# A four-layer graph kernel whose instruction order is planned: weight preparation put into the plan, and planned times as occupancies

## The chip, the cores and the metric

The kernel runs on one core of a Trainium2 chip. The metric is the device time of one execution in microseconds (us). All times below come from the profile of the kernel before, or from its timed runs.

## The reference

32 graphs of 512 nodes with 256 features pass through four layers, each followed by a residual and a layer norm over the features. Everything is float32. `A` is the weighted adjacency matrix (512 x 512) of a graph.

```python
# layer 0: a graph isomorphism layer
h = (1.0 + eps) * x + einsum('bnm,bmd->bnd', adj, x)
x = layernorm(x + relu(h @ W1 + b1) @ W2 + b2)
# layer 1: graph attention, 4 heads of 64
h = einsum('bnd,dhf->bnhf', x, W)
e = leaky_relu(e_dst[:, :, :, None] + e_src[:, :, None, :], 0.2)   # e_src, e_dst: h times a_src, a_dst
attn = softmax(where(adj > 0.5, e, -1e9))
x = layernorm(x + einsum('bhij,bjhf->bihf', attn, h) + bias)
# layer 2: attention, 8 heads of 32
scores = q k^T / sqrt(32) + log(adj + 1e-6)                          # q, k, v: x times Wq^T, Wk^T, Wv^T
x = layernorm(x + (softmax(scores) v) @ Wo^T + bo)
# layer 3: attention of x on itself, one head
s = (x @ W) x^T * adj, masked by the node mask
x = layernorm(x + softmax(s) x)
```

## The kernel before

**A plan.** Each graph is a list of some 330 steps. A step (class `Step`) has a name, an engine, a planned time in us, the steps that it comes after, the buffers that it takes, and a tiling mode of TensorE (`row`, `c32`, `c64`, or none). `Plan.order` plays a list schedule in advance, while the program is built: of the steps that can start first (within `ahead` us), it takes the one with the earliest due time. The due time of a step of graph g is `g * period` less the planned length of the longest chain behind it (`Plan.link`), plus `stay` times the planned cost of a change of tiling (table `CHANGE`). A planned time carries a hop after it: 0.2 us on TensorE, 0.05 on others (`HOP`). `Plan.run` tries 30 settings of `(period, ahead, window, stay)`, keeps the one whose plan ends first, and emits the steps in that order. Each engine then runs its own instructions in that order, and waits only where its operands demand it. The setting kept before is period 30, ahead 0.15, window 5, stay 100.

**Buffers.** 14 large ones (`B`, 8 KB per partition), 13 medium ones (`C`, 4 KB), and 8 PSUM banks (`p`). Counters in the same dictionary limit the number of graphs in a phase: `live` 5 graphs in all, `L0` to `L3` in the layers.

**The prologue** stands outside of the plan, and ahead of it (lines 244 to 365). ACT issues 24 DMAs for the weights; the four square weights are transposed on TensorE (L299) and evacuated by ACT (L304); DVE makes `selfw` (the identity times 1 + eps, L277) and the two extra columns of `wg_sb` (L284, L285); then two bounds are computed, one for the offsets of layer 1 (L311 to L327) and one from the Gram matrices of the q and k weights (L341 to L365). They decide at the end whether the result may be off limits, in which case a general path runs; with these inputs it doesn't. The temporaries of the prologue use the buffers C0 to C9.

**Steps of a graph**, by name, with the lines of the profile:

- layer 0: `at` transposes of A (L503), evacuated by ACT (`ate`, L511) and DVE (`atd`, L507); `h` (L535, `he` L542), `f` (L558, `fe` L564), `y` (L577), residual and norm `x1`, `st1` (L465, L423), `ve`, `dev`, `sh`, `r` (L436, L441, L446, L454).
- layer 1: `xt1` (L603), `v1` (L624, `ve1` L630), the bound offsets enter in `ab` (L638); the rows `R` go to DRAM and come back on all partitions as `R_bc` (`Rd`, L675); `z` (ACT, L714), `zm` (DVE, L725), `o1` (L748, mode c64); the sums of the weights through accumulating DMAs (L776) into `d1` (L794, c32); `yt` (L813 to L815), `yn`, `st2`.
- layer 2: `xt2` (L854), `q` and `k` (L873), `v2` (L891); for each of eight pairs of head group and column block, `s` (L910, mode row: 4 heads at once), `e` (ACT, L923), `m` (DVE, L932), `n` (L968, c32); the E tiles are added up by accumulating DMAs (`cd`, L943) into `d2` (L992, c32), whose reciprocal (`rc`, L1007) scales the output before `p` (L1040).
- layer 3: A is loaded again; `xt3`, `i` (L1079), `t` (L1093), `ta`, `tb` (DVE, L1107, L1113), `te` (ACT, L1121), `u` (L1138, `ue` L1147), `w` (L1165), `wx` (L1179), and the store.

Five graphs are under way at a time, so that TensorE's matmuls of one graph fill the waits of another.

Of the kernel before, what the change touches and what calls it, by code (L numbers as in the profile page):

```python
# [16 lines left out]
P = 128  # L17
# [28 lines left out]
class Plan:  # L46
# [6 lines left out]
    HOP = {"pe": 0.2}  # L53
# [19 lines left out]
    def step(self, name, eng, us, after=(), take=(), free=(), mode=""):  # L73


        def add(emit):
            steps = self.steps[-1]
            assert name not in steps and all(a in steps for a in after), (name, after)
# [17 lines left out]
    def link(self):  # L96

        self.left = []
        for steps, frees in zip(self.steps, self.frees):
            for name, s in steps.items():  # L100
                for a in s.after:
                    steps[a].then.append(name)
            for k, (_, after) in enumerate(frees):
                for a in after:
                    steps[a].frees.append(k)
            left = {}
            for name in reversed(steps):
                s = steps[name]
                left[name] = s.us + max(
                    (left[n] + self.HOP.get(s.eng, 0.05) for n in s.then), default=0.0  # L110
                )
            self.left.append(left)

    def order(self, period, ahead, window, stay):
# [9 lines left out]
        todo = [len(steps) for steps in self.steps]  # L124

        def open_to(n):
            nonlocal opened
            while opened < min(n, len(self.steps)):
                for name, s in self.steps[opened].items():
                    if not s.after:  # L130
                        ready[opened, name] = 0.0
                opened += 1

        open_to(window)
        while low < len(self.steps):
            found = []
            for (g, name), t in ready.items():
# [8 lines left out]
                else:  # L146
                    due = g * period - self.left[g][name] + stay * change
# [15 lines left out]
            end = ends[g][name] = t + s.us + (self.HOP.get(s.eng, 0.05) if s.eng else 0.0)  # L163
            last = max(last, end)
            out.append((g, name, t, got))
            for n in s.then:
                waits[g][n] -= 1
                if not waits[g][n]:
                    after = self.steps[g][n]
                    ready[g, n] = max(  # L170
                        ends[g][a] - (self.HOP.get(after.eng, 0.05) if after.eng == self.steps[g][a].eng and after.eng else 0.0)
                        for a in after.after
                    )
            for k in s.frees:
                fwaits[g][k] -= 1
                if not fwaits[g][k]:
                    key, after = self.frees[g][k]
                    kind, i = held[g].pop(key)
                    room[kind].append((max(ends[g][a] for a in after), i))
# [18 lines left out]
def fast_path(  # L198
# [39 lines left out]
    turn = [0]  # L238

    def bank_of(shape, name):  # L240
        turn[0] += 1
        return ps.tile(shape, F32, tag=f"p{turn[0] % 8}", name=name)

# [4 lines left out]
    nc.gpsimd.memset(nhalf, -0.5)  # L248
    ones = const.tile([P, P], F32, name="ones")
# [3 lines left out]

    w1_sb = const.tile([P, DC, DH], F32, name="w1_sb")
    nc.scalar.dma_start(w1_sb, w1.rearrange("(c p) f -> p c f", p=P))
    w2_sb = const.tile([P, HC, D], F32, name="w2_sb")
    nc.scalar.dma_start(w2_sb, w2.rearrange("(c p) f -> p c f", p=P))
    b1_sb = const.tile([P, HC], F32, name="b1_sb")
    nc.scalar.dma_start(b1_sb, b1.rearrange("(c p) -> p c", p=P))

    wg_sb = const.tile([P, DC, VW], F32, name="wg_sb")
    nc.scalar.dma_start(wg_sb[:, :, :D], wg.rearrange("(c p) h f -> p c (h f)", p=P))
    w3_sb = const.tile([P, DC, D], F32, name="w3_sb")
    nc.scalar.dma_start(w3_sb, w3.rearrange("(c p) f -> p c f", p=P))

    biases = dram.tile([3, NC, D], F32, tag="biases", name="biases", bufs=1)
    for k, b in enumerate((b2, gbias, bo)):
        for c in range(NC):
            nc.scalar.dma_start(biases[k, c : c + 1], bass.AP(b.tensor, b.offset, [[0, 1], [1, D]]))
    eps_bc = const.tile([P, 1], F32, name="eps_bc")  # L270
    nc.scalar.dma_start(eps_bc, row_bcast(eps0, 1))


    eps1 = const.tile([P, 1], F32, name="eps1")
    nc.vector.tensor_scalar_add(eps1, eps_bc, 1.0)
    selfw = const.tile([P, P], F32, name="selfw")
    nc.vector.tensor_scalar_mul(selfw, ident, eps1)  # L277

    for k, (name, a) in enumerate((("src", a_src), ("dst", a_dst))):
        a_bc = sb.tile([P, D], F32, tag=f"C{k}", name=f"a_{name}")  # L280
        nc.scalar.dma_start(a_bc, row_bcast(a, D))
        prod = sb.tile([P, DC, D], F32, tag=f"C{k+2}", name=f"wa_{name}_prod")
        for c in range(DC):
            nc.vector.tensor_mul(prod[:, c, :], wg_sb[:, c, :D], a_bc)  # L284
        nc.vector.tensor_reduce(  # L285
            wg_sb[:, :, D + k * H1 : D + (k + 1) * H1],
            prod.rearrange("p c (h f) -> p c h f", h=H1), AX.X, ALU.add,
        )


    wT = {}
    for i, (name, w) in enumerate((("q", wq), ("k", wk), ("v", wv), ("o", wo))):
        raw = sb.tile([P, DC, D], F32, tag=f"C{i+4}", name=f"w{name}_raw")
        nc.scalar.dma_start(raw, w.rearrange("(c p) f -> p c f", p=P))
        wT[name] = const.tile([P, DC, D], F32, name=f"w{name}T")
        pt = bank_of([P, N], f"w{name}_t")
        for ci in range(DC):
            for co in range(DC):
                nc.tensor.transpose(  # L299
                    pt[:, ci * D + co * P : ci * D + (co + 1) * P],  # L300
                    raw[:, co, ci * P : (ci + 1) * P],
                    ident,
                )
# [896 lines left out]
    for g in range(B):  # L1200
        graph(g)
# [475 lines left out]
```

## Time and profile before

| | |
|---|---|
| time, median of 3 runs | 3109.85 us (3102.59 to 3111.73) |
| span of the profiled run | 3097.9 us |
| TensorE matmuls (PE) | 2988.1 us busy, 15053 records |
| VectorE (DVE), ScalarE (ACT), GpSimd (POOL) | 2035.1, 1920.6, 617.1 us busy |
| DMA | 500.83 MB, mean 162 GB/s |
| mean granted clock of TensorE | 0.984 |
| first matmul of a graph starts at | 32.77 us |
| last matmul starts, its row's end | 3079.09, 3086.2 us |

A record of TensorE is one pass of a float32 matmul; a matmul of 512 columns is two. Busy times are unions: records that overlap count once. The time behind "idle before" is that in which the engine had nothing running, put down to what ended it. A release named "DMA" is a transfer's landing. Matmuls are pipelined, so a busy TensorE can still be losing time between two starts.

### The profile page before, as it was taken

To read this page: it belongs to the slowest core of one execution; us is meant where nothing else is said; L and a number is where in the kernel's file an instruction comes from. 1 tells how busy PE (TensorE), PEld (TensorE's weight loads), DVE (VectorE), ACT (ScalarE), POOL (GpSimd) and SP (SyncE) were. 2 spreads that over 40 slices of the span, in tenths; PEclk is the share of its full clock that TensorE was granted. 3 is DMA by queue.
4 is the path that set the end of the run, shared out by engine and by line. 5 is a ranking of instruction groups with operands and counts; after the bars stand their busy time and mean duration, and the time that the engine had idled before them with its cause. 6 is when DMAs were issued, how large, how long until landed. Compare 5 with 4: busy or idle time off the path is not lost.

```text
span 3097.9 us, 41135 instructions
## 1 busy us (share of the span) xinstructions
PE 2988.1 (96%) x15053; PEld 1698.5 (55%) x15053; DVE 2035.1 (66%) x3935; ACT 1920.6 (62%) x3849; POOL 617.1 (20%) x686
## 2 busy tenths in 40 slices
PE   6989999999999999999999999999999999999886
PEld 5545565555555555555555565555555555555443
DVE  1566666776576677666676666676576676666664
ACT  2656756666666566666666756666666567656552
POOL 1221221221122221122221121221221221122210
PEclk9999999999999999999999999999999999999898
DMA  4686877786877777777877877786877777776753
GB/s 133 146 182 143 169 171 155 174 174 159 182 157 162 172 162 180 167 148 169 179 162 171 170 170 155 177 171 154 179 164 162 167 167 177 175 149 147 175 124 69
DMA packets 160143, 500.83 MB, mean 162 GB/s; under 512 B 13504, under 2 KB 49088, under 8 KB 131264
## 3 DMA queue, kind: packets, MB, share of 16 engines
q0 software_dynamic: 78336, 352.36, 59.3%
q1 hardware_dynamic: 77824, 142.88, 13.6%
q10 hardware_dynamic: 3776, 2.90, 0.3%
q8 instruction: 121, 1.98, 0.2%
q14 instruction: 86, 0.70, 0.1%
HBM read 179.06 MB, written 17.05 MB: 63 GB/s over the span
## 4 chain that ended last, share of the span: by engine, by line
PE 75%; DMA 10%; ACT 9%; DVE 4%; issue 2%; ACTq 0%; POOL 0%; SPq 0%; POOLq 0%
PE s L910 8%; PE o_ps L1165 7%; PE o_ps L748 6%; PE hT_ps L535 6%; PE o_ps L968 6%; ACT z L714 6%; DMA R_bc<-R_dram 5%; PE y_ps L577 5%; PE v_ps L624 4%; PE kT_ps L873 4%; PE o2p_ps L1040 4%; PE iT_ps L1079 4%; PE v_ps L891 4%; PE qT_ps L873 4%; PE h1T_ps L558 3%; PE s L1093 3%
## 5 line engine op out<-in xcount | busy, mean ns | idle before, releaser
L932 DVE SCALAR_TENSOR_TENSOR z<-AT,z 128x1024 f32<-128x1024 f32 x512 | 602.9, 1222 | 481.7 <-ACT z L923 481.7
L923 ACT ACTIVATE z<-s 128x512 f32<-128x512 f32 x1024 | 525.3, 611 | 141.4 <-PE s L910 141.4
L943 POOL DMA_DIRECT2D z<-z x192 | 171.7, 899 | 1390.0 <-PE o_ps L968 504.8
L714 ACT ACTIVATE z<-R_bc,nT,S 128x512 f32<-128x512 f32 x512 | 377.9, 805 | 108.5 <-DMA R_bc<-R_dram 94.1
L725 DVE SCALAR_TENSOR_TENSOR z<-z,T,edge 128x512 f32<-128x512 f32 x512 | 349.9, 746 | 137.4 <-ACT z L714 137.4
L454 ACT ACTIVATE x<-x,shift,rstd 128x256 f32<-128x256 f32 x512 | 277.4, 596 | 228.8 <-DVE shift L446 222.2
L776 POOL DMA_DIRECT2D z<-z x256 | 224.6, 938 | 555.6 <-PE o_ps L748 317.9
L910 PE MATMUL s<-qT,kT 32*128 32x512 f32 x2048 | 284.9, 633 | 0.0
L968 PE MATMUL o_ps<-z,v 128*32 128x512 f32 x2048 | 262.5, 600 | 0.1
L577 PE MATMUL y_ps<-w_sb,h1T 128*128 128x256 f32 x1024 | 244.6, 392 | 13.6 <-ACT h1T L564 13.2
L748 PE MATMUL o_ps<-z,v 128*64 128x512 f32 x1024 | 242.3, 608 | 10.7 <-DVE z L725 6.3
L1093 PE MATMUL s<-xT,iT 128*128 128x512 f32 x512 | 240.2, 600 | 0.0
L558 PE MATMUL h1T_ps<-hT,w_sb 128*128 128x512 f32 x512 | 238.1, 599 | 0.0
L1165 PE MATMUL o_ps<-x,eT 128*128 128x256 f32 x1024 | 231.3, 383 | 0.0
L577 PEld LDWEIGHTS y_ps<-w_sb,h1T 128*128 128x128 f32 x1024 | 192.6, 194 | 66.5 <-ACT h1T L564 26.3
L1007 DVE RECIPROCAL rdT<-rdT 128x256 f32<-128x256 f32 x128 | 213.5, 1716 | 12.5 <-ACT rdT L1000 12.5
L1165 PEld LDWEIGHTS o_ps<-x,eT 128*128 128x128 f32 x1024 | 192.8, 191 | 48.4 <-ACT yT L761 8.1
L423 DVE BATCH_NORM_STATS2 st<-x 128x6 f32<-128x256 f32 x512 | 211.0, 412 | 6.0
L535 PE MATMUL hT_ps<-AT,x 128*128 128x384 f32 (+2 forms) x768 | 209.4, 382 | 0.0
L441 POOL TENSOR_TENSOR rstd<-ve,nhalf 128x4 f32<-128x4 f32 x128 | 148.2, 1158 | 262.8 <-DVE ve L436 237.5
L910 PEld LDWEIGHTS s<-qT,kT 32*128 32x128 f32 x2048 | 86.2, 183 | 162.9 <-issue 68.2
L1093 PEld LDWEIGHTS s<-xT,iT 128*128 128x128 f32 x512 | 94.4, 190 | 131.1 <-issue 108.6
(149 smaller groups left out, 4260.7 us busy)
## 6 DMA issues: line engine op xcount, KB each, us to landing
z<-z POOLq DMA_DIRECT2D x192, 1024.0 KB, 8.4
A<-in_adj_dram SPq DMA_DIRECT2D x64, 1024.0 KB, 6.7
z<-z POOLq DMA_DIRECT2D x128, 512.0 KB, 8.3
x<-biases POOLq DMA_DIRECT2D x96, 512.0 KB, 6.8
R_bc<-R_dram SPq DMA_DIRECT2D x32, 1024.0 KB, 7.9
z<-z POOLq DMA_DIRECT2D x128, 256.0 KB, 7.3
x<-in_x_dram SPq DMA_DIRECT2D x32, 512.0 KB, 3.4
out_dram<-x SPq DMA_DIRECT2D x32, 512.0 KB, 3.0
```

The lines of the kernel that those rows point to most:

```text
L535: nc.tensor.matmul(ph[:, cols], t["x"][:, m, blk(d)], moving, start=(k == 0), stop=(k == len(parts) - 1),)
L558: nc.tensor.matmul(ph, w1_sb[:, d, blk(f)], t["hT"][:, d, :], start=(d == 0), stop=(d == DC - 1))
L577: nc.tensor.matmul(py[:, j, :], t["h1T"][:, f, blk(2 * c2 + j)], w2_sb[:, f, :], start=(f == 0), stop=(f == HC - 1),)
L714: nc.scalar.activation(t[f"e{h}"][:, c, :], t["Rbc"][:, h, :], AF.Relu, bias=t["nT"][:, h, c : c + 1], scale=t["S"][:, h, c : c + 1],)
L725: nc.vector.scalar_tensor_tensor(z, z, t["T"][:, h, c : c + 1], t["edge"][:, c, :], op0=ALU.add, op1=ALU.mult)
L748: nc.tensor.matmul(po[j * F1 : (j + 1) * F1, :], t["v"][:, c, h * F1 : (h + 1) * F1], t[f"e{h}"][:, c, :], start=(c == 0), stop=(c == NC - 1),
L910: nc.tensor.matmul(pk, t["k"][hs, o, blk(c)], t["q"][hs, o, :], start=True, stop=True)
L923: nc.scalar.activation(t[f"E{k}"][:, j, :], t[f"ps{k}{j}"], AF.Exp, scale=QSCALE)
L932: nc.vector.scalar_tensor_tensor(z, t["AT"][:, c, None, :].to_broadcast([P, 2, N]), ADJ_EPS, z, op0=ALU.add, op1=ALU.mult,)
L968: nc.tensor.matmul(t[f"n{o}"][32 * j : 32 * j + 32, :], t["v2"][:, c, o * P + F2 * j : o * P + F2 * (j + 1)], t[f"E{k}"][:, j, :], start=( ...
L1093: nc.tensor.matmul(pt, t["iT"][:, d, blk(c)], t["xT3"][:, d, :], start=(d == 0), stop=(d == DC - 1),)
L1165: nc.tensor.matmul(py[:, j, :], t["eT"][:, m, blk(2 * c2 + j)], t["x"][:, m, :], start=(m == 0), stop=(m == NC - 1),)
```

## The change

The weight loads, weight transposes and bounds become steps of the plan, as a graph of their own ahead of the others (`prepare`); steps of the graphs name them with a `^`. So their place in each engine's order is planned, and the first graph's loads no longer follow them. The planned times of ACT and DVE become occupancies, the time in which the engine is held, and what a dependent step waits beyond it is a hop: to another engine (`HOP`) or to the next step on the same one (`BACK`). Two graphs may be in layer 2 at once (`L2`), and six under way (`live` and the window). The due times can be shifted by a fixed random amount for each step name. No matmul, activation or vector operation of a graph is changed.

```diff
-    HOP = {"pe": 0.2}
+    HOP = {"pe": 0.2, "act": 0.15, "dve": 0.13, "pool": 0.05, "sp": 0.05}
+    BACK = {"act": 0.13, "dve": 0.12}
...
+    def hop(self, a, b):
+        if a.eng == b.eng:
+            return self.BACK.get(a.eng, 0.0)
+        return self.HOP.get(a.eng, 0.0)
...
-    def order(self, period, ahead, window, stay):
+    def order(self, period, ahead, window, stay, shift=0.0, seed=0):
...
+        rng = random.Random(seed)
+        moved = {n: rng.uniform(-shift, shift) for n in [*self.steps[0], *self.steps[-1]]}
...
-                    due = g * period - self.left[g][name] + stay * change
+                    due = max(g - 1, 0) * period - self.left[g][name] + moved[name] + stay * change
...
-        "live": 5, "L0": 1, "L1": 2, "L2": 1, "L3": 1, "AT": 4, "zs": 7,
+        "live": 6, "L0": 1, "L1": 2, "L2": 2, "L3": 1, "AT": 4, "zs": 7,
...
+    def prepare():
+        plan.graph()
...
+        def load(name, us, *transfers, take=()):
+            @step(f"ld_{name}", "act", 0.5 * len(transfers), take=take)
+            def _():
+                for transfer in transfers:
+                    nc.scalar.dma_start(*transfer())
+            @step(name, "q3", us, (f"ld_{name}",))
+            def _():
+                pass
...
+            @step(f"wt{name}", "pe", 0.44, (f"raw{name}",), take=(f"p=wt{name}",))
...
+            @step(f"we{name}", "act", 0.49, (f"wt{name}",), free=(f"wt{name}",))
...
+        load("bias", 3.0, *(bias_rows(k, b) for k, b in enumerate((b2, gbias, bo))))
...
+        @step("wa", "dve", 3.2, ("wg",), take=("C=prod",), free=("prod", "a0", "a1"))
...
+        for o in range(DC):
+            @step(f"gr{o}", "pe", 1.0, ("weq", "wek"), take=(f"p=gr{o}0", f"p=gr{o}1"))
...
-                f"f{f}", "pe", 1.72, row("he", DC) + prev("f", f),
+                f"f{f}", "pe", 1.72, row("he", DC) + prev("f", f) + ("^w1",),
...
-            @step(f"fe{f}", "act", 0.72, (f"f{f}",), free=(f"f{f}",))
+            @step(f"fe{f}", "act", 0.58, (f"f{f}",), free=(f"f{f}",))
...
-                @step(f"z{h}{c}", "act", 0.62, ("Rl", "ST") + prev(f"z{h}", c), take=() if c else (f"B=z{h}",))
+                @step(f"z{h}{c}", "act", 0.7, ("Rl", "ST") + prev(f"z{h}", c), take=() if c else (f"B=z{h}",))
...
-                    f"e{k}{j}", "act", 0.66, (f"s{k}",) + prev(f"e{k}", j),
+                    f"e{k}{j}", "act", 0.51, (f"s{k}",) + prev(f"e{k}", j),
...
-                @step(f"m{k}{i}", "dve", 1.25, (f"e{k}{2*i+1}",) + prev(f"m{k}", i))
+                @step(f"m{k}{i}", "dve", 1.14, (f"e{k}{2*i+1}",) + prev(f"m{k}", i))
...
+    prepare()
     for g in range(B):
         graph(g)
     with tc.manual_schedule():
-        plan.run([(p, a, 5, b) for p in range(25, 45, 5) for a in (0.0, 0.15, 0.3) for b in (0.0, 100.0)])
+        plan.run([(28, 0.0, 6, 100.0, 8.0, 34035), (28, 0.05, 6, 30.0, 3.0, 427523), (28, 0.0, 6, 15.0)])
```

The first of the three settings is the one that the plan keeps. The three loads of a bias replace twelve, one for each of its four copies.

## The prediction

> **What bounds the kernel now.** First the page: busy time of each engine.
>
> ```profile
> ## 1 busy us (share of the span) xinstructions
> PE 2988.1 (96%) x15053; PEld 1698.5 (55%) x15053; DVE 2035.1 (66%) x3935; ACT 1920.6 (62%) x3849; POOL 617.1 (20%) x686
> ```
>
> TensorE is the bound; 110 us of the span is left beside it, and the next engine has a third of its time free. Second, the busy time by stage (core, stretch, sums, granted clock, DMA share, GB/s): prologue, filling, steady stretch, and two pieces of the emptying.
>
> ```profile
> 0.00:33.00 33.00, 8.07 (x46) 7.20 (x47) 6.62 (x31) 4.36 (x9) 4.99 (x14) 0.92 0.47 148
> 33.00:260.00 227.00, 214.64 (x1039) 129.09 (x1039) 113.53 (x227) 131.88 (x254) 44.65 (x49) 0.96 0.65 145
> 260.00:2800.00 2540.00, 2515.06 (x12794) 1428.41 (x12796) 1728.26 (x3336) 1627.78 (x3272) 521.66 (x573) 1.00 0.76 168
> 2950.00:3098.00 148.00, 112.64 (x488) 61.28 (x484) 79.41 (x149) 60.61 (x125) 14.24 (x16) 0.87 0.43 94
> ```
>
> Idle by the first number (PE): 25 us in the prologue, 12 in the filling, 25 in 2540 us of steady work, and 35 in the last 148. So the steady stretch has 1% idle; the two ends have half of all of it.
>
> Third, the chain of waits at the start (start, length, what).
>
> ```profile
> 25.41 0.20 ACT gg L346
> 25.61 0.02 issue
> 25.63 0.44 SPq L478
> 26.07 0.06 issue
> 26.13 6.60 DMA A<-in_adj_dram
> 32.73 0.04 issue
> 32.77 3.67 PE AT_t L503 x16
> ```
>
> The first x load waits for the bound computation of the prologue (a shared C buffer), and graph 0 starts at 32.8 us. Fourth, TensorE's waits in 260 to 2960 us (total, times, longest).
>
> ```profile
> PE y_ps L577 <- ACT h1T L564: 13.2, 21, 0.9
> PE eT_t L1138 <- ACT z L1121: 13.1, 13, 6.0
> PE d_ps L992 <- DMA z<-z: 4.4, 1, 4.4
> PE o_ps L748 <- ACT eT L1147: 4.3, 9, 0.6
> ```
>
> Fifth, a piece of TensorE's timeline across changes of its tiling, and sixth the end (start, length).
>
> ```profile
> 1006.22 1.14 PE L910 MATMUL s<-qT,kT 32*128 32x512 f32 x8
> 1007.29 1.92 PE L968 MATMUL o_ps<-z,v 128*32 128x512 f32 x16
> 1009.15 1.14 PE L910 MATMUL s<-qT,kT 32*128 32x512 f32 x8
> ```
> ```profile
> 3029.04 1.06 PE L968 MATMUL o_ps<-z,v 128*32 128x512 f32 x8
> 3044.43 1.39 PE L992 MATMUL d_ps<-z,ones 128*32 128x512 f32 x8 [2.58 <-DMA z<-z]
> 3050.59 6.01 PE L1040 MATMUL o2p_ps<-woT,yT 128*128 128x256 f32 x16 [4.77 <-DVE yT L1011]
> ```
>
> Untiled matmuls of 512 columns start 0.43 us apart (L558: 16 take 6.87 us in the chain). The sixteen of L968 are four groups of four at once, 4 x 0.43 = 1.72, but the next step starts after 1.86. By the start times of single matmuls in the steady stretch, the one before a change of tiling lasts 0.09 us too long on entering a tiling or leaving the row tiling, and 0.11 on leaving a column tiling. These 0.1 us count as busy, so the page's 96% hides them.
>
> **What the Trainium skill says.** "TensorEngine Tiling (Array Packing)", Key Properties: a change of the tiling mode, not of the tile alone, drains TensorE. It gives no price; the trace agrees and gives 0.09 to 0.11 us. "TensorE: Matmul & The Clock Gate", Part 1: after an idle window of about 3.4 us the array runs at half clock until it has been busy that long. Agreed: mean clock 0.87 in the last 148 us, and the 16 matmuls of L1040 there take 6.0 us, against 3.46 at 0.216 each in the steady stretch. "DMA: Bandwidth & Descriptors", Queues, rings and completion order: the rows of SP and ACT are served in turn by the same 16 DMA engines. No single row of before shows both queues loaded at once; I use it for the start below.
>
> **The change part by part.**
>
> *Prologue.* Loads on SP now lead: x and A of graph 0 need no C buffer of the prologue, and are issued at about 0.8 and 1.2 us, where the ACT queue now has its first issue. Before, A landed 7.1 us after SP's first issue. Lower end for the landing: 0.8 + 7.1 = 8. Upper end: the ACT queue (2.9 MB of weights, now 15 issues instead of 24, about 0.5 us each) takes half of the engines, so that 2 x 1.6 MB pass before A is there; the stretch from 30 to 42 us moved 350 to 390 GB/s, which gives 9 us, with 2 us of latency (w1 alone: 0.5 MB in 3.8 us) and the issue 12. I take 10, so graph 0 starts 22.8 us sooner. The second A needs 4.7 MB of SP loads and 2.9 MB of weights, 7.6 MB at 0.36 MB/us and 2 us: about 23 us, where TensorE wants it at 10 + 11 = 21 (the distance in before from 32.8 to 43.7): 0 to 3 us of waiting, and I take 0, since w3 and the last weights come after. Against that, the weight transposes (16), bounds and gram products (29 more records) now stand in TensorE's planned stream: 45 x 0.11 = 4.9 us. Net 17.9; ends 13 and 20. What goes with them elsewhere costs nothing: 6.6 us of DVE and 4.4 of ACT in the prologue row move beside TensorE's work, on engines with a third free; the issues on ACT end at about 8 us, before its first copy of AT.
>
> *Order of TensorE.* The list of instructions of both programs has the same matmuls: no work is added or removed. Changes of tiling fall from 783 to 697. 86 x 0.1 = 8.6 us; ends 7.7 and 9.7.
>
> *Waits in the steady stretch.* Occupancies in place of durations change no instruction, only what the planner thinks free. I measured the slack that the new order leaves: the TensorE work (rows at 0.43 per 512 columns) standing between a step and the one that needs its result. From f3 to y0 (L558 to L577) the median goes from 1.7 to 7.4 us; the evacuation between takes 0.68 (L564) and its hops, so the 13.2 us can go. From n3 to d20, which waits for the three collecting DMAs, 18.3 becomes 27.9: 4.4 go. From t3 to u0 8.7 becomes 8.6: the 13.1 stay, and so do the 4.3 of L748. New thin places: h1 to f0 6.9 becomes 1.8 and d1 to yt0 7.9 becomes 2.7, each above the one evacuation (0.59 and 0.69) that it must cover, if ACT is not behind. Sum 17.6; I take 15. Behind a wait on TensorE stands everything, as its queue runs in order. Ends: 0 and 25.
>
> *Two graphs in layer 2, six under way.* No buffer is added; this is what makes the longer distances possible (s7 to n7: 6.9 to 41). Its price is that E tiles live longer. I cost it at nothing more, as the slack above is measured with it.
>
> *End.* From n7 of the last graph to its p0 before has u, w and d2: 1.76 + 6.92 + 1.72 = 10.4 us of work in 3050.59 - 3030.04 = 20.5 us (the matmul after n7 starts at 3030.04), 10 lost. After, i, t, u, d2 and w of the graph before stand there: 3.44 + 6.88 + 1.76 + 1.72 + 6.92 = 20.7, enough. But the last graph's s and n now have less to stand beside, and its four exps a step (4 x 0.51 = 2.05 us) are longer than s and n (1.8). I take 8; ends 3 and 12. The 12 us from the last matmul to the end stay.
>
> Sum: 17.9 + 8.6 + 15 + 8 = 49.5; 3109.85 - 49.5 = 3060.
>
> **The rivals.** *Plan too tight.* Longer planned times were slack: with occupancies, late DMAs (R_bc lands in 4.2 to 13.1 us, planned as 8.5) reach TensorE. For it: ACT already waits 94 us for R_bc. Against: the distances grew. Start and tilings hold, waits and end bring nothing: 3109.85 - 26.5 = 3083. *Loads collide at the start.* Both A late, start worth 7 instead of 18: 3071. *New wait in each graph.* The longer lives of E, or ACT running behind the plan at the thin places, cost 2.5 us per graph, 32 x 2.5 = 80, and 10 us of half clock; less 26.5 + 8: 3165, slower. Against: ACT and DVE have a third free. *All goes.* The waits of the steady stretch and its half clock vanish, and the filling loses its 12 us of idle too: 3035.
>
> **How the numbers follow.** Forecast (3060) 0.62; too tight (3083) 0.15; collision (3071) 0.06; all goes (3035) 0.12; new wait (3165) 0.05. The range leaves out the slow case and the outer ends of the others: 3032 to 3092. Faster by over 0.3% (below 3100): all but the slow case and the upper edge of the tight one, 0.92; within 0.3%: 0.03; slower: 0.05.
>
> **What would show it.** Start: the first AT_t at 8 to 12 us, and the transposes of wq between matmuls of graphs. Tilings: adjacent out transfers of the steady stretch, now 93.2 us apart on average (417.7 to 2841.3 us, 26 graphs), about 92 apart. Waits: no y_ps on h1T row. End: p0 of the last graph with under 2 us of idle before it. Wrong: a new row among TensorE's waits of over 30 us, above all one on z from ACT or DVE or on a DMA; or AT_t waiting for A for long past 12 us.

## The result, and the profile after

| | before | after |
|---|---|---|
| time, median | 3107.1 us (4 runs beside after) | **3012.0 us** (4 runs, 3010.7 to 3013.0) |
| ratio after to before | | **0.9693**, 95% interval 0.9676 to 0.9711 |
| span of the profiled run | 3097.9 us | 3011.3 us |
| TensorE: mean granted clock, changes of tiling | 0.984, 783 | 0.991, 697 |

The change makes the kernel 95 us faster. 49.5 were forecast, and the time lies under the range. The profiled execution of before was one of its shorter ones, so that the two profiles differ by 86.6 us; the account below is of those. (One correction to the kernel before as told above: the plan tries 4 x 3 x 2 = 24 settings, not 30.)

The page of after, busy time of each engine:

```profile
## 1 busy us (share of the span) xinstructions
PE 2944.1 (98%) x15053; PEld 1703.7 (57%) x15053; DVE 2009.7 (67%) x3935; ACT 1946.5 (65%) x3849; POOL 619.8 (21%) x686
```

TensorE has the same 15053 records, and is still the bound; its busy time fell by 44 us, and its idle time by 43. Stages of after, in the columns of the table shown for before (stretch, length, busy time of PE, PEld, DVE, ACT, POOL, granted clock, DMA share, GB/s); the last row ends with the span, as the one of before did:

```profile
0.00:33.00 33.00, 12.56 (x58) 10.58 (x59) 2.18 (x12) 3.94 (x7) 0.96 (x10) 1.00 0.78 263
33.00:260.00 227.00, 212.49 (x1054) 124.44 (x1052) 123.48 (x261) 133.85 (x267) 51.24 (x55) 0.95 0.66 141
260.00:2800.00 2540.00, 2537.12 (x13096) 1473.96 (x13095) 1748.26 (x3417) 1694.59 (x3350) 536.26 (x587) 1.00 0.79 170
2865.00:3012.00 147.00, 117.45 (x503) 62.67 (x502) 83.38 (x170) 64.48 (x132) 15.99 (x17) 0.91 0.48 108
```

The third row carries the result: 25 us of idle in the steady stretch have become 2.9, and 302 more records of TensorE fit into the same 2540 us. The first row shows that the earlier start is worth little: 12.6 us busy in 33, against 8.1. TensorE's waits of after from 260 to 2870 us (total, times, longest) are three rows:

```profile
PE y_ps L713 <- ACT h1T L700: 2.2, 1, 2.2
PE d_ps L1128 <- DMA z<-z: 0.6, 1, 0.6
PE o2p_ps L1176 <- DVE yT L1147: 0.5, 1, 0.5
```

L713 is L577 of before. Its 21 waits of 13.2 us have become one of 2.2.

**Where the 86.6 us came from.** TensorE's work in a graph is the same, so the two traces can be laid side by side by work done: each record of a matmul counted at its undisturbed spacing (0.43 us for 512 columns, four small tiles at once counted as one), the preparation of weights left out. Full work is some 2834 us. The rows depend a little on these spacings: with slightly smaller ones, 2778 us of work in all and the limits of the rows moved in proportion, the three gains come out at -4, 66 and 25 us. So they hold to some 5 us.

| stretch, by TensorE's work done | before | after | gain |
|---|---|---|---|
| start and filling, to 400 us of work | 467.0 | 467.5 | -0.5 |
| steady, 400 to 2650 us of work | 2377.0 | 2316.4 | 60.6 |
| emptying, from 2650 to the end | 253.9 | 227.4 | 26.5 |

The steady row holds some 25.5 graphs. Per graph, worked out from the start times of the matmuls (a stall is a start over 15 ns late without recorded idle, a change of tiling or half clock; some 0.1 us each, and counted as busy; half clock is half of the time at that clock, idle inside it included):

| us per graph | before | after |
|---|---|---|
| matmuls at their own spacing | 88.26 | 88.24 |
| changes of tiling | 2.22 | 1.90 |
| waits (with the late start after them) | 1.29 | 0.09 |
| half clock | 0.39 | 0.06 |
| stalls | 1.17 | 0.69 |
| rest | -0.10 | -0.13 |
| sum | 93.22 | 90.84 |

Out transfers of before are 88 to 100 us apart. In after they are 90.5 us apart in each of 24 graphs from 538.9 to 2711.5 us: the order repeats itself from graph to graph, and no graph meets a late buffer.

What became of the loads of R_bc, which all 32 graphs need? The answer on that tile: what ended ACT's idle time before it (us, times), and the last line of it. First before, then after.

```profile
  DMA R_bc<-R_dram: 94.1, 22
...
DMA to landing us min/median/max: 4.2/7.9/13.1
```
```profile
  DMA R_bc<-R_dram: 17.8, 5
...
DMA to landing us min/median/max: 4.2/4.5/9.3
```

The same megabyte lands in 4.5 us instead of 7.9. No step of the forecast has it, and most of the experiments are about it.

### The profile page after: what moved, and what is told of

It is laid out like the page before. It is cut to its first block, busy times and chain, and to the rows that moved or that the text cites. A ratio compares the mean times of both kernels' runs of the same rounds, so it can differ in the third digit from the quotient of the medians.

```text
span 3011.3 us, 40812 instructions
## 1 busy us (share of the span) xinstructions
PE 2944.1 (98%) x15053; PEld 1703.7 (57%) x15053; DVE 2009.7 (67%) x3935; ACT 1946.5 (65%) x3849; POOL 619.8 (21%) x686
## 5 line engine op out<-in xcount | busy, mean ns | idle before, releaser
L1068 DVE SCALAR_TENSOR_TENSOR z<-AT,z 128x1024 f32<-128x1024 f32 x512 | 610.9, 1217 | 273.2 <-ACT z L1059 272.7
L1059 ACT ACTIVATE z<-s 128x512 f32<-128x512 f32 x1024 | 551.3, 611 | 268.3 <-PE s L1046 268.1
L861 DVE SCALAR_TENSOR_TENSOR z<-z,T,edge 128x512 f32<-128x512 f32 x512 | 357.8, 747 | 62.2 <-ACT z L850 62.0
L850 ACT ACTIVATE z<-R_bc,nT,S 128x512 f32<-128x512 f32 x512 | 382.1, 819 | 17.8 <-DMA R_bc<-R_dram 17.8
L590 ACT ACTIVATE x<-x,shift,rstd 128x256 f32<-128x256 f32 x512 | 295.4, 602 | 108.0 <-DVE shift L582 108.0
L912 POOL DMA_DIRECT2D z<-z x256 | 228.8, 1033 | 467.5 <-DMA z<-z 265.2
L1046 PE MATMUL s<-qT,kT 32*128 32x512 f32 x2048 | 291.8, 634 | 0.1
L577 POOL TENSOR_TENSOR rstd<-ve,nhalf 128x4 f32<-128x4 f32 x128 | 134.7, 1052 | 696.9 <-DVE ve L572 671.6
L713 PE MATMUL y_ps<-w_sb,h1T 128*128 128x256 f32 x1024 | 232.4, 381 | 2.2 <-ACT h1T L700 2.2
L884 PE MATMUL o_ps<-z,v 128*64 128x512 f32 x1024 | 230.8, 602 | 1.5 <-DVE z L861 1.5
L713 PEld LDWEIGHTS y_ps<-w_sb,h1T 128*128 128x128 f32 x1024 | 194.6, 191 | 52.8 <-issue 20.7
L1046 PEld LDWEIGHTS s<-qT,kT 32*128 32x128 f32 x2048 | 93.5, 183 | 158.7 <-issue 66.8
L694 PEld LDWEIGHTS h1T_ps<-hT,w_sb 128*128 128x128 f32 x512 | 90.5, 190 | 122.0 <-issue 112.8
```

What stands on the lines that cost most here:

```text
L590: nc.scalar.activation(t["x"][:, c, :], t["x"][:, c, :], AF.Identity, bias=t["shift"][:, c : c + 1], scale=t["rstd"][:, c : c + 1],)
L694: nc.tensor.matmul(ph, w1_sb[:, d, blk(f)], t["hT"][:, d, :], start=(d == 0), stop=(d == DC - 1))
L713: nc.tensor.matmul(py[:, j, :], t["h1T"][:, f, blk(2 * c2 + j)], w2_sb[:, f, :], start=(f == 0), stop=(f == HC - 1),)
L850: nc.scalar.activation(t[f"e{h}"][:, c, :], t["Rbc"][:, h, :], AF.Relu, bias=t["nT"][:, h, c : c + 1], scale=t["S"][:, h, c : c + 1],)
L861: nc.vector.scalar_tensor_tensor(z, z, t["T"][:, h, c : c + 1], t["edge"][:, c, :], op0=ALU.add, op1=ALU.mult)
L884: nc.tensor.matmul(po[j * F1 : (j + 1) * F1, :], t["v"][:, c, h * F1 : (h + 1) * F1], t[f"e{h}"][:, c, :], start=(c == 0), stop=(c == NC - 1),
```

## The experiments

In all of them before took 3106 to 3109 us beside the kernel. In the tables, the plan's own end is what `Plan.order` reckons for the order that is kept: 3024.5 us for before, 2965.0 for after (the prologue of before and of s4 is not in it, and before, e4 and s2 reckon with the old planned times).

### One part undone, at one fixed setting

The first theory was that each part of the change brings a share. The setting of after (first of its three) carries a random shift of the due times; e1 takes the shift away, and e2 to e4 undo one more thing each at that same setting.

```diff
e1  -  plan.run([(28, 0.0, 6, 100.0, 8.0, 34035), ...
    +  plan.run([(28, 0.0, 6, 100.0)])
e2  +  plan.run([(28, 0.0, 6, 0.0)])                 # stay 0
e3  +  plan.run([(28, 0.0, 5, 100.0)])  "live": 5, "L2": 1
e4  +  plan.run([(28, 0.0, 6, 100.0)])  planned times and hops of before
```

> The changed kernel without the random shift of due times (setting 28, 0.0, 6, 100.0 alone); its order has 690 changes of tiling, the changed kernel's 697. Three theories on the 2.7 us per graph that the steady stretch won: S, the shift found an order without waits; L, two graphs in layer 2 and six under way give each step other work to stand behind; O, occupancies make the plan true. S: most of the waits are back, 3060 us or more, out transfers about 93 us apart. L or O: 3005 to 3030 us, under 91.5 us apart.

> As e1_no_shift, with the weight of a change of tiling set from 100 to 0; 1079 changes instead of 690, the same matmuls. If a change costs its 0.1 us of TensorE time, 389 x 0.1 = 39 us longer than e1_no_shift, and 1.2 us per graph in the steady stretch. If the drain is hidden (TensorE waits anyway), within 10 us of e1_no_shift.

> As e1_no_shift, with the limits of before: one graph in layer 2, five under way (window 5). 832 changes of tiling, which alone are 14 us over e1_no_shift. L: the waits of before return, 3080 us or more. O or S: only the tilings show, e1_no_shift plus 10 to 20 us.

> As e1_no_shift, with the planned times and hops of before (durations, 0.05 us after an ACT or DVE step, none between steps of one engine). 748 changes of tiling, 6 us over e1_no_shift. O: the waits of before return, 3070 us or more. L: e1_no_shift plus 0 to 15 us.

| | time, us | plan's own end | ratio to before | largest wait of TensorE |
|---|---|---|---|---|
| e1_no_shift | 3300.4 | 3074 | 1.0619 (1.0601 to 1.0636) | xT_t on ACT's x: 81.0 us, 41 times |
| e2_no_stay | 3257.2 | 3018 | 1.0481 (1.0463 to 1.0498) | AT_t on the load of A: 91.1, 18 |
| e3_no_limits | 3265.8 | 3147 | 1.0511 (1.0493 to 1.0528) | d_ps on the accumulating DMAs: 111.9, 16 |
| e4_no_occ | 3185.0 | 3066 | 1.0238 (1.0213 to 1.0263) | iT_ps on ACT's xT: 62.1, 7 |

The theory fell. With every part in place and the shift alone removed, the kernel is 288 us slower than after, slower than before too, and taking any part away then makes it faster. The plan itself reckons 109 of e1's 288 us; the rest it does not know of. An order that another draw gives differs by more than any part is worth, so nothing about a part follows from these runs. e2 has 389 changes of tiling more than e1 and is faster by 43 us; it prices nothing.

### One part undone, each with the best of 4000 settings

To be fair to each variant, its setting was searched for: the best of 4000 random ones by the plan's own end.

```diff
s1  all parts         plan.run([(28, 0.05, 6, 100.0, 3.0, 464227)])
s2  old planned times plan.run([(28, 0.05, 6, 30.0, 3.0, 4473)])
s3  L2 1, live 5      plan.run([(30, 0.0, 5, 30.0, 8.0, 958237)])
s4  prologue of before, outside of the plan
                      plan.run([(28, 0.0, 6, 100.0, 3.0, 589598)])
```

> The changed kernel with another setting: the one whose plan ends first among 4000 random ones (period 26, 28 or 30, ahead 0 or 0.05, weight of changes 30 or 100, shift 3 or 8, any seed): 28, 0.05, 6, 100, 3, 464227. Its order repeats from graph to graph, with 744 changes of tiling. If the parts of the change allow an order without waits and a search finds one, 3000 to 3030 us with out transfers about 91 us apart; if the setting of the changed kernel was a rare hit, 3060 us or more.

> As s1_all, but with the planned times and hops of before, and the best of the same 4000 settings by its own plan (28, 0.05, 6, 30, 3, 4473; 848 changes of tiling). If occupancies matter because the plan must be true for its best order to be the chip's best, TensorE's waits return: 3060 us or more. If they do not matter, s1_all plus the tilings, 10 us.

> As s1_all, but with one graph in layer 2 and five under way, and the best of the same 4000 settings with window 5 (30, 0, 5, 30, 8, 958237; 896 changes of tiling, 15 us over s1_all). If two graphs in layer 2 and six under way are what frees the steady stretch, 3060 to 3090 us, as fast as the kernel before less its start; if the search alone does it, 3015 to 3045 us.

> As s1_all, but with the prologue of before ahead of the plan, and the best of the same 4000 settings (28, 0, 6, 100, 3, 589598; 744 changes of tiling). If the start is worth what the forecast said, s1_all plus 18 us. If it is given back in the filling, as the traces of before and of the changed kernel suggest (100 us of matmul work are done at 141 and at 145 us), s1_all plus 0 to 5 us, with its first matmul of a graph at about 33 us.

| | time, us | plan's own end | ratio to before |
|---|---|---|---|
| s1_all | 3227.0 | 2961 | 1.0379 (1.0355 to 1.0402) |
| s2_no_occ | 3045.6 | 2975 | 0.9791 (0.9770 to 0.9812) |
| s3_no_limits | 3096.7 | 3006 | 0.9959 (0.9938 to 0.9980) |
| s4_no_prologue | 3083.9 | 2959 | 0.9913 (0.9891 to 0.9935) |

Again each variant is one draw, and again all three with a part undone beat the one with all parts, so the table prices no part. But s1 has the same parts as after, and the plan holds its order to be as good (2961 us against 2965), yet the chip takes 215 us longer. So the plan is wrong about something that decides. s1's largest waits of TensorE say where, and ACT's what stands behind it (total, times, longest):

```profile
PE y_ps L713 <- ACT h1T L700: 154.6, 23, 10.6
```
```profile
ACT z L850 <- DMA R_bc<-R_dram: 246.2, 31, 13.5
```

TensorE waits for h1T of one graph, an evacuation that takes ACT 0.6 us. It is late because it stands in ACT's queue behind z of another graph, and z waits for R_bc: one late load holds the whole of ACT. In the trace of s1 each of the 23 waits ends within 9 us of such a stand of ACT for R_bc, of 5.8 to 13.5 us. One of them, on ACT's timeline (start, length, what; idle before it in brackets); TensorE's y_ps starts at 556.4 us, after 5.9 us of idle:

```profile
550.71 5.04 ACT L850 ACTIVATE z<-R_bc,nT,S 128x512 f32<-128x512 f32 x7 [8.69 <-DMA R_bc<-R_dram]
555.66 0.66 ACT L700 ACTIVATE h1T<-h1T_ps,b_sb 128x512 f32<-128x512 f32 x1
```

s2, with the longer planned times of before, repeats every 91.5 us; that these times act as slack against a late load is how I read it, and no run shows it.

ACT's wait for R_bc goes with the time in most runs: 3 to 27 us in f4, after and s2, 81 to 110 in s4, before, s3 and e4, 165 to 246 in e1, f6, d2 and s1. The exceptions are d1 (4.9), e3 (33.2) and e2 (84.5), slow orders whose largest waits of TensorE are for other transfers. A rival to the load's lateness is the slack that meets it. The TensorE work between f3 and y0, counted as in the prediction, has a median of 7.3 us in after and f4 and 9.5 in s2, the three fastest orders, and of 4.3 or less in every other order tried (3.4 in s1, 1.7 in before). The next runs change the load and leave the order, and so the slack, as it is.

### R_bc, the load in question

d1 lets the plan reckon with 12.5 us for R_bc (best setting of 4000 again); d2 keeps the order of after and issues the load twice; the second issue stands 4.7 us after the first. In d2 z waits for R_bc in all 32 graphs, and starts 14.4 us (median) after the first issue, where after's load has landed 4.5 us after its own: some 10 us later.

```diff
d1  -  @step("Rl", None, 8.5, ("Rd",))
    +  @step("Rl", None, 12.5, ("Rd",))
       plan.run([(28, 0.05, 6, 100.0, 3.0, 691195)])
d2     nc.sync.dma_start(R_bc.rearrange("p h n -> p (h n)"), row_bcast(R_dram, H1 * N))
    +  nc.sync.dma_start(R_bc.rearrange("p h n -> p (h n)"), row_bcast(R_dram, H1 * N))
```

> The changed kernel with one planned time altered: the way of R to DRAM and back (step Rl) 12.5 us instead of 8.5, and again the best of the same 4000 settings by its own plan (28, 0.05, 6, 100, 3, 691195; 661 changes of tiling). New theory D: what the plan has wrong is the landing of R_bc, which shares the DMA engines with the accumulating transfers (median 4.5 us in the changed kernel, 9.7 in s1_all, to which 3.6 to 5.9 us for writing R come); ACT then stands at z, and the evacuations behind it hold TensorE. D: 3000 to 3030 us, ACT waits under 60 us for R_bc. If the orders are good or bad by chance in other ways: as likely over 3050 us as s1_all was.

> The changed kernel in its own order, with the load of R_bc issued twice in a row into the same tile, so that z starts one landing later, 4 to 5 us per graph, and 1 MB more is moved per graph. D: ACT waits for R_bc 100 us or more in total, and the time rises by 30 to 130 us. If the order has slack there: within 15 us of the changed kernel.

d2 took 3203.4 us (1.0305, 1.0288 to 1.0322): 191 us above after, more than expected, and 6 us a graph for a load some 10 us later. ACT's wait came straight back:

```profile
ACT z L851 <- DMA R_bc<-R_dram: 234.8, 32, 16.1
```

So after's order, with its slack of 7.3 us, doesn't bear such a delay; it needs R_bc early as well. TensorE's largest wait in d2 is elsewhere, 58.1 us of s in layer 3 on ACT's iT: a stand of ACT is felt in more places than y0. (d2 also moves 1 MB more in each graph, which this run doesn't part from the delay.) d1 took 3166.3 us (1.0187, 1.0170 to 1.0203), 61 us under s1, but far from the 3000 to 3030 of its theory. R_bc left the top of ACT's waits, and another transfer took its place at TensorE, the accumulating DMAs of layer 1, some 2.6 us in most graphs:

```profile
PE d_ps L930 <- DMA z<-z: 67.2, 26, 3.3
```

### A quarter of R_bc, each order kept

Three runs load R_bc for head 0 alone, and all four heads read that row, so layer 1's output is another one; orders stay.

```diff
-  nc.sync.dma_start(R_bc.rearrange("p h n -> p (h n)"), row_bcast(R_dram, H1 * N))
+  nc.sync.dma_start(R_bc[:, 0, :], row_bcast(R_dram, N))
-      t[f"e{h}"][:, c, :], t["Rbc"][:, h, :], AF.Relu,
+      t[f"e{h}"][:, c, :], t["Rbc"][:, 0, :], AF.Relu,
```

> The kernel of s1_all, with its order kept, but R_bc is loaded for head 0 alone (0.26 MB written instead of 1.05 MB) and all four heads read that row; so layer 1's output is not the reference's. Theory A (the late landing of R_bc behind which ACT's queue stands is what this order loses on): the landing falls from 9.7 to about 4 us, ACT's wait for R_bc from 246 to under 60 us, TensorE's wait for h1T from 155 to under 30, and the time from 3227 to about 3080, at most 3130. Theory B (another resource takes its place): R_bc lands early, but a wait on the accumulating DMAs or on another evacuation follows, and the time stays above 3160.

> The kernel before, with its order kept, R_bc loaded for head 0 alone as in f1_thin_s_all (layer 1's output is not the reference's). Theory A: ACT's wait for R_bc, 94 us before, goes; TensorE loses its 13 us on h1T and the stalls and half clock that follow on them: about 3085, between 3065 and 3095; out transfers about 92.3 us apart. Theory C (before loses its 2.7 us a graph by the unevenness of its order, whatever the loads do): within 8 us of 3107.

> The changed kernel, with its order kept, R_bc loaded for head 0 alone as in f1_thin_s_all (layer 1's output is not the reference's). Theory A: this order no longer loses anything on R_bc, so the time stays within 6 us of 3012, and out transfers stay 90.5 us apart. Theory B: less DMA traffic helps other transfers as well, and the time falls below 3000.

| | time, us | against the same order, full load | ACT's wait for R_bc |
|---|---|---|---|
| f1_thin_s_all | 3169.2 | 3227.0 | 190.9 (from 246.2) |
| f2_thin_before | 3061.7 | 3108.5 | 36.3 (from 94.1) |
| f3_thin_after | 3008.4 | 3012.0 | 10.4 (from 17.8) |

f2 is the run that prices it: before's own order gains 47 us between the medians when R_bc is a quarter as long, more than expected. The two profiles differ by 38, as that of before was one of its shorter executions. By the table of work done, 36 of those are in the steady stretch (2377.0 to 2340.7), where a graph falls from 93.22 to 91.79 us: waits 1.29 to 0.34, half clock 0.39 to none. None is in the emptying (253.9 to 255.2). The rows of f2 for y_ps, 13.2 us in before, and for R_bc:

```profile
PE y_ps L577 <- ACT h1T L564: 6.9, 10, 0.9
ACT z L714 <- DMA R_bc<-R_dram: 36.3, 15, 5.2
```

The runs of before, with the full load, lie between 3102.8 and 3114.7; the four of f2 within 1.5 us. f3 shows that after has next to nothing left to gain there (3.6 us), and that the smaller traffic is worth little by itself in that order. f1's time is that of its theory B, but not for B's reason: the landing fell only from 9.7 to 6.8 us, and ACT kept most of its wait for R_bc. So the bytes of R_bc are not all of it.

**What makes it late.** Ahead of the load, the rows R go to DRAM, 8 KB, and the load waits for them. Single transfers in the traces of before, after, s1 to s4, d1, f2, f4 and f6 (those whose landings are recorded, with no other transfer of SP under way at the issue) give for these 8 KB:

| accumulating DMAs of GpSimd under way at the issue | writes | landing, us: median (range) |
|---|---|---|
| none | 18 | 1.4 (1.3 to 2.9) |
| one | 86 | 3.1 (1.3 to 7.1) |
| two or more | 61 | 4.8 (2.4 to 6.4) |

And from this write's issue to R_bc's landing, median: after 6.1 us (13 of 20 graphs with none under way), f4 8.5, s3 9.4, e1 10.9, s4 11.1, s2 11.4, d1 and before 12.4 (in before 31 of 32 with one or more), f6 12.8, s1 17.0 (19 of 21 with two or more). The plan takes 8.5 in all of them but d1, f4 and f6. So it has a fixed time for a chain of two transfers whose length goes with what the order puts beside it; after's order puts it mostly into the gaps of the accumulating DMAs. This is a count over traces: no run moved the accumulating DMAs alone. And the length of the chain alone doesn't rank the orders: s2's is 11.4 us and s3's 9.4, but s2, with the larger slack, is 51 us faster. That the DMA engines share themselves out between the queues is what the Trainium skill says ("DMA: Bandwidth & Descriptors", Queues, rings and completion order: each engine goes round the rows that have work, a packet at a time); it gives no price for it; the table here is one, as a count.

### The plan told the truth, and the limits undone in it

f4 is after with three planned times of transfers raised to what the traces show, and the best of 4000 settings. f6 is f4 with one graph in layer 2 and five under way.

```diff
f4, f6  -  @step("Rl", None, 8.5, ("Rd",))
        +  @step("Rl", None, 12.5, ("Rd",))
        -  @step(f"as{h}{k}", None, 2.5, (f"aq{h}{k}",))
        +  @step(f"as{h}{k}", None, 5.0, (f"aq{h}{k}",))
        -  @step(f"cs{k}", None, 2.5, (f"cq{k}",))
        +  @step(f"cs{k}", None, 5.0, (f"cq{k}",))
f4         plan.run([(30, 0.05, 6, 100.0, 3.0, 34613)])
f6         plan.run([(28, 0.05, 5, 30.0, 8.0, 628893)])  "live": 5, "L2": 1
```

> The changed kernel with three planned times of transfers raised to what the traces show: Rl from 8.5 to 12.5, the last part of an accumulating DMA (as, cs) from 2.5 to 5.0; the setting is the best of 4000 random ones by its own plan, (30, 0.05, 6, 100.0, 3.0, 34613). Theory A (the plan chooses badly because its transfer times are too short, so truthful ones mend it): below 3060, with no wait of TensorE over 30 us. Theory D (no fixed time is right, since a landing depends on what else is moved, and which order repeats well is luck of the draw): above 3090, with a wait of TensorE on some transfer or on an evacuation behind one.

> f4_truth with one graph in layer 2 and five under way, as before; setting the best of 4000 random ones by its own plan, (28, 0.05, 5, 30.0, 8.0, 628893). If the second graph in layer 2 and the sixth under way are what pays for transfers planned at their real length, then this loses 3 us a graph or more against f4: above 3080, with a wait of TensorE that comes each graph, or out transfers more than 93 us apart. If the transfers' planned times were all that was wrong (s3_no_limits, 3097, lost on them), it comes within 25 us of 3014.

f4 took **3014.1 us** (0.9698, 0.9675 to 0.9721), 213 us under s1, which differs by three planned numbers and the setting that the search then chose. It has 690 changes of tiling, and its out transfers are 90.5 us apart too, in another order than after's. On its tile R_bc:

```profile
  DMA R_bc<-R_dram: 3.1, 1
...
DMA to landing us min/median/max: 4.9/6.5/7.5
```

The load is not as early as in after. It is planned for, and ACT waits for it once. So planned times near those of the traces led to an order as good as after's, whose plan (2983 us) and time lie 31 us apart, against 266 in s1. It is one draw all the same; how often such times give a good order wasn't tried.

f6 took 3282.6 us (1.0566, 1.0549 to 1.0584), 268 us above f4. Its out transfers alternate between 67 and 131 us, it has 1001 changes of tiling, and TensorE waits for A, which is issued when d1 of another graph has ended and lands 18 to 20 us later (total, times, longest):

```profile
PE AT_t L639 <- DMA A<-in_adj_dram: 82.2, 14, 9.3
```

Most of the loss is foreseen: the plan's own end is 3159 us, against 2983 for f4. So with transfers planned near their real length, 4000 draws gave no order for five graphs that covers them, where six graphs had one; in this pair the second graph in layer 2 and the sixth under way pay. s1 against s3 had the opposite sign; that both were planned on transfers that didn't come is how I read it. (One setting each; the best that the plan finds in 4000.)

### The start

d3 keeps after's order, and lets GpSimd issue the weight loads, but for eps, w1, b1 and the biases. d4 and f5 do so in d1 and f4, with these issues planned on GpSimd as well.

```diff
+  queue = nc.scalar if name in ("eps", "w1", "bias") else nc.gpsimd
   for transfer in transfers:
-      nc.scalar.dma_start(*transfer())
+      queue.dma_start(*transfer())
```

> The changed kernel in its own order, with the loads of w2, wg, a_src, a_dst, the four square weights and w3 issued by GpSimd instead of ACT. In the changed kernel ACT issues its last load at 22.2 us, each issue held until an earlier transfer has landed, and TensorE stands 8.8 us for the first copy of AT. If that wait is worth its length: 8 to 9 us less, about 3003 us. If it is given back in the filling, as the rest of the start was: within 3 us of 3012.

> d1_rl_all and d3_pool_loads together. If both hold, 8 us under d1_rl_all, and the fastest of all if d1 is at or under the changed kernel; if the start is given back, the same as d1_rl_all.

> f4_truth with the weight loads, but for eps, w1, b1 and the biases, issued by GpSimd as in d3_pool_loads (planned on it too); the same setting. If what d3 showed holds for another order, ACT's first copies start some 7 us sooner, A lands some 3 us later, and the time is 3 to 6 us under f4's 3014: about 3009, which would stand beside d3's 3007.5. If the order's own waits take it up, it stays at 3014.

They took 3007.5 (0.9677, 0.9661 to 0.9693), 3153.9 (1.0150, 1.0133 to 1.0167) and 3007.7 us (0.9680, 0.9664 to 0.9696): some 4.5, 12.5 and 6 us under their pairs. Why, ACT's start in after shows (start, length, what; idle before it in brackets):

```profile
3.90 0.57 ACTq L320 DMA_DIRECT2D biases<-in_L_gnn_bias_dram  x1
6.56 0.57 ACTq L320 DMA_DIRECT2D biases<-in_L_gnn_bo_dram  x1
10.81 0.37 ACTq L320 DMA_DIRECT2D w_sb<-in_L_gnn_W_dram  x1
...
19.05 0.53 ACTq L320 DMA_DIRECT2D rawo<-in_L_gnn_Wo_dram  x1
22.17 0.38 ACTq L320 DMA_DIRECT2D w_sb<-in_L_gnn_W_dram  x1
22.58 1.28 ACT L647 ACT_TABLE_LOAD   x1 [22.58 <-DMA a<-in_L_gnn_a_dst_dram]
23.87 2.05 ACT L647 COPY AT<-AT_t 128x512 f32<-128x512 f32 x4
```

From the sixth on, an issue uses a semaphore (a completion counter) that an earlier transfer has, and stands until that one has landed (w1 landed at 10.79; the next issue is at 10.81). Eight such counters go round among the loads of SP and ACT, so ACT stands for SP's loads too. ACT's first copy stands behind the last of them. In d3 it starts at 16.57 instead of 23.87. A lands later there, so the net is less than the 8.8 us of TensorE's wait that go:

```profile
PE AT_t L640 <- DMA A<-in_adj_dram: 17.0, 2, 15.1
```

d3 and f5 are the fastest kernels of the study that compute the reference's output, some 4 us under after. Two different orders end within 0.3 us of each other.

## Why the prediction was wrong, step by step

**The bound, and that no work is added: right.** The matmuls' own spacing is 88.26 and 88.24 us a graph.

**Start, 17.9 forecast, -0.5 measured (with the filling): wrong.** A at 8 to 12 us was right: the first AT_t starts at 11.60, a lead of 21.2 us. The moved preparation, 4.9 forecast, costs 4.3. The step that failed is "the issues on ACT end at about 8 us, before its first copy of AT". They end at 22.6. From the first AT_t to 400 us of work, TensorE's recorded idle rose from 12.6 to 24.0 us. The rows of after behind it, none of them there before once its first graph had begun:

```profile
PE hT_ps L671 <- ACT AT L647: 8.8, 1, 8.8
...
PE qT_ps L1009 <- ACT xT L994: 5.2, 2, 4.8
PE fmt L493 <- DVE fmax L488: 4.8, 1, 4.8
...
PE gg L472 <- DVE gm L466: 2.5, 1, 2.5
```

Two of them, gg and fmt, are the chain of the bound, which I had costed by its TensorE records alone: in TensorE's own queue a chain of small steps through other engines costs their latency as well. The rest of the lead went to stalls (5.1 to 9.0 us), half clock (1.5) and small terms.

**Tilings, 8.6 forecast: right.** 2.22 to 1.90 us a graph, some 8 us in the 25.5 steady graphs.

**Waits in the steady stretch, 15 forecast; 51 came: the step that failed most.** Waits gave 1.20 us a graph, 30.6 in all; half clock 0.33, 8.4; stalls 0.48, 12.2. Three mistakes in it. I took the idle of the page's waits, and left out what a wait brings after it. I kept 13.1 us of eT_t on z as steady waits that stay, and all of them went: 6.5 are steady, and 6.7 lie after 2844 us, in the emptying, into which my window of 260 to 2960 reached (as do the 4.4 us of d_ps). And I asked which distances on TensorE grew, but not why h1T was late. R_bc's 94 us of ACT's waiting stood in the prediction, in a rival and with the wrong sign (new planned times would make it worse). In before the 20 longest of the 21 waits for h1T each come 2.8 to 16.4 us after ACT has stood 2.9 to 8.0 us for R_bc; one, on ACT's timeline:

```profile
1127.56 2.23 ACT L714 ACTIVATE z<-R_bc,nT,S 128x512 f32<-128x512 f32 x3 [3.08 <-DMA R_bc<-R_dram]
1129.69 0.67 ACT L564 ACTIVATE h1T<-h1T_ps,b_sb 128x512 f32<-128x512 f32 x1
```

f2 shows that three quarters of R_bc cost before's order 36 us of its steady stretch. Of the other 24 us that after gains there, the tilings are 8, and the table has some 10 in stalls and 6 in waits; what in the order brings these stays open. The slack from f3 to y0, 7.4 us in place of 1.7, was rightly seen as a help: the fast orders have it and s1, which waited 154.6 us there, has 3.4. But d2 shows that it doesn't suffice when R_bc is late.

**End, 8 forecast, 26.5 measured: too small.** The piece that I reckoned gave at most 2 us. In after, 29.5 us lie between the matmul behind n7 and the p0 that waits, with 21.1 us of work in them: 8.4 lost, where 10 were in before. And the idle ahead of p0 didn't change: 4.77 before, 4.81 after (start, length, what):

```profile
2957.57 1.06 PE L1128 MATMUL d_ps<-z,ones 128*32 128x512 f32 x8 [0.28 <-DMA z<-z]
2958.56 0.70 PE L1176 MATMUL o2p_ps<-woT,yT 128*128 128x256 f32 x2
2964.08 6.06 PE L1176 MATMUL o2p_ps<-woT,yT 128*128 128x256 f32 x14 [4.81 <-DVE yT L1147]
```

The work that I had placed there does stand in between, but that wait is for DVE's yT, behind the reciprocals, and I had counted only the distance from n7. The gain came from elsewhere: from 2650 us of work to the end, TensorE's recorded idle fell from 34.9 to 18.0 us, 17 of the 26.5. Half clock took 47.8 us of it in before, 19.6 of them idle, and 17.1 in after, 2.4 of them idle (up to the last matmul); the busy part runs at half its pace (a record of L1138 every 0.21 us in place of 0.11), which costs some 14 and 7 us. In before two waits stood close together, and half clock was granted from 2881.2 to 2898.3:

```profile
2882.89 1.93 PE L992 MATMUL d_ps<-z,ones 128*32 128x512 f32 x8 [4.41 <-DMA z<-z]
2890.82 0.48 PE L1138 MATMUL eT_t<-ident,z 128*128 128x128 f32 x1 [6.00 <-ACT z L1121]
```

What in after's order removed such waits from the end was not tried; f2 shows that a smaller R_bc does not. The Trainium skill's idle window before half clock ("TensorE: Matmul & The Clock Gate", Part 1), which the prediction quoted for the end alone, lies close to these two waits: half clock was granted 2.7 us into the first. It is not the whole of it: in before's steady stretch half clock also followed waits of 1.1 us (granted from 1034.6 and from 2430.6, but not after the one at 1871.3), and in after twice no pause over 0.07 us (from 262.9 and 2921.9). The measurement decides here.

**The sum.** -0.5 + 60.6 + 26.5 = 86.6 in place of 49.5; the other 8.6 us of the timed 95 are before's profiled execution, which was shorter than its median. *All goes* (3035) was the nearest rival, and right on the steady stretch, though for a cause that it didn't name. *Plan too tight* was wrong for after and right for s1 and d1: with the same parts and other settings late transfers did reach TensorE, at 121 and 59 us over before. What I called "planned times as occupancies" is not priced by these runs; the order that the setting gives decides, and the prediction's measure of an order was its distances on TensorE alone. More was at hand: which graph's z stands ahead of which evacuation on ACT, and which accumulating DMAs stand before R's write.

**What would show it.** Two of the four signs came as told (AT_t at 11.6 us; the row y_ps on h1T all but gone). Out transfers are 90.5 us apart, not 92. p0's idle stayed. No new row of 30 us appeared.

**Open.** How the kept setting was found, the code doesn't say. f4 is one draw in which planned times near the traces' sufficed, and d1 one in which lengthening R_bc alone didn't; which of the two lengthened accumulating steps was needed wasn't tried. The stalls of 0.1 us, fewer in after (8 a graph against 15), were only counted. How much of after's gain is the early load and how much the slack behind it, the runs don't part.

## What to carry to other kernels

A list schedule is only as good as its planned times: before searching settings, compare each planned transfer, whole chains included, with its landing in the trace, and search only then (here three numbers and a new draw were worth 213 us). An engine that runs in order hands a late load on to everything behind it, so follow a wait of the bound engine to the head of the releasing engine's queue; the instruction named in the wait is often not the late one. And don't judge a part of such a change with the setting held fixed: another draw moved the time by more than any part.

## What the runs showed of the hardware that was not expected

- An 8 KB write to DRAM from SP's queue lands in 1.4 us with no accumulating DMA of GpSimd under way, and in 3.1 and 4.8 us (medians, single ones up to 7.1) beside one and two.
- An engine's DMA issues are not free for what it computes: in this program ACT's 15 weight loads, some 0.5 us each, took until 22.6 us, as later issues wait for earlier transfers to land, SP's among them.
- Two pauses of TensorE of 4.4 and 6.0 us in before, 8 us apart, were followed by half clock for 17.1 us (2881.2 to 2898.3). Of these 6.7 us were idle; the other 10.4 ran at half their pace and lost some 5 us on top of the pauses.
- Half clock came in after also where TensorE's row shows no pause over 0.07 us: from 262.9 us, after 3 us in which the tiled matmuls of s started one or two at a time, up to 0.5 us apart, where they start four at once elsewhere.
